# The opening of a decoder layer: one weight write earlier, GpSimd in program order, and the feed-forward buffers placed elsewhere

## The chip, the cores and the metric

The kernel runs on one core of a Trainium2 chip. The metric is the device time of one execution in microseconds, and a kernel's time is the median of its runs. TensorE (PE) multiplies matrices, VectorE (DVE), ScalarE (ACT) and GpSimd (POOL) work elementwise, and SyncE (SP) issues the transfers.

## The reference, cut to what matters

The input `x` has four time steps of 2048 items with 512 features, and there is a context of 77 rows for each of the four steps. Everything is in fp32. Three residual branches follow one another, each on a layer norm of x:

```python
def reference(x, ctx, ...):
    x = x + recurrence(layernorm(x), ...)      # 4 steps; z = V (A z + Vinv_dt u_t), per block of 64; 2 Re z
    x = x + cross_attention(layernorm(x), ctx, Wq, Wk, Wv, Wo)   # 16 heads of 32, 77 keys, softmax
    x = x + ffn(layernorm(x), ...)
    return x

def ffn(x, W_exp, b_exp, up_weights, up_bias, down_weights, W_con, b_con, down_bias):
    h = x @ W_exp + b_exp                      # 512 -> 2048
    h = butterfly(h, up_weights, 2048)         # 11 stages of 2x2 mixes
    h = gelu(h + up_bias)                      # exact
    h = butterfly(h, down_weights, 2048)
    return h @ W_con + b_con + down_bias       # 2048 -> 512
```

No weight meets a data-dependent value before the products, so the kernel composes each butterfly with its dense matrix once, and the recurrence of four steps becomes four fixed 64x64 taps.

## The kernel before, in words

**The rounds.** The 2048 items are worked in 16 groups of 128, each with its four time steps: 512 rows. `front(u)` makes the two norms, the recurrence and the attention of group u; `feed_forward(u)` makes its feed-forward part. After an opening, round u runs `feed_forward(u)`, and its `step()` calls draw pieces of `front(u+1)` in between, so that TensorE always has products of the one while the elementwise engines work on the other. The big products go by a seven-product scheme for 2x2 blocks: each matrix is kept as seven combinations of its quarters. There are seven for the query weights (`wq`, written to DRAM as `wq7`, and loaded again in every later round), seven for the output weights (`wo`, kept in SBUF), seven for each of eight column pieces p of the first feed-forward matrix (`up7[p]`), and seven arrays `dn7` for the second.

**The opening.** It prepares the operands and runs `front(0)`, and it is written as three generators that `run(...)` advances by hand in a fixed order:

- `_recurrence_taps` (L111 to L134) makes the taps `gt`: each step multiplies into a PSUM bank `ps_g` (then VectorE copies it out, L117), and into `ps_rr` and `ps_ri`, from which VectorE makes the next power. `_keys_values` (L140 to L160) loads the context `ct` and the weights `wk` and `wv`, multiplies the keys `ps_k` (L148; VectorE places them into `kbd`, L152) and the values `ps_v`.
- `_prepare` ("prep") composes the butterflies with the dense matrices. It regroups factors through DRAM (`hp_dn`, L218), multiplies diagonal pieces (L248 on VectorE), makes `wup`, the composed first matrix, and from its quarters the operands `up7[p]`: three of them are quarters as they are and are written straight from `wup` (L331, 24 DMA issues), four are sums made by two GpSimd and two VectorE operations for each p (L335 to L338) in a slot of the buffer `wo` (three slots, p % 3) and written from there (L339, eight DMA issues). Then the second matrix is composed into the same `wup` (L346, 16 groups of matmuls, each evicted by ScalarE or VectorE), transposed or multiplied on in the pairs L356 and L365, and its sums (L377 on VectorE and others) are written to `dn7`.
- `front(0)` ("first"): the norm (bn_stats; L469 on VectorE makes rows `xp`, L480 on TensorE transposes them into `ps_t`), the recurrence (L510), the second norm (L442 makes `xn`, L451 transposes), the query product (L495, whose partial sums VectorE adds in L532), the scores (L553), their softmax (L557, L558 on VectorE, L559 exp on ScalarE, L561 the sum, L563 the scaling on GpSimd), the transposes of the probabilities (L575 into `ps_pt`; the copies to SBUF, `pt`, by ScalarE in L578 and by VectorE in L580), the products with the values (L585) and with the output weights (L495 again, into `ps_w`), and the norm for the feed-forward.

**Buffers that are shared.** In SBUF `pt` has one buffer, and the query weights `wq` lie in the same one: it is free for the probabilities only when `wq` has been written out to `wq7` (L812) and the copy has landed. `wk` shares a buffer with `bd` of prep. The coefficients' pools (`prep`: `wup`, `wdn` and others) are released at the end of the opening, and the pools of the feed-forward (`ffn`, and `wts` with three buffers for weights in flight) are allocated after that. PSUM has eight banks named by tags; a new tile of a tag waits until the previous user of that bank has been read. `ps_g`, `ps_rr` and `ps_ri` all use tag f, as do the transposes and scores; prep uses a, b and c.

**What sets the order.** In the opening TensorE and SP run in program order (`tc.manual_schedule(engines={E.PE, E.SP})`); on the other engines, and on all of them in the rounds, a scheduler orders the instructions by when it thinks their inputs are ready. An engine works strictly through its queue: an instruction that waits stops what stands behind it. DMAs are issued from SP's queue, and take eight semaphores in turn, so each waits also for the one eight before it.

**Around the end of the opening.** The first weights `w_up` of the feed-forward are loaded at L663 and first used at L654. The operands of the right side, `tb` among them, are made by `combine` (L624, L625). The biases `ybias` are loaded and added on GpSimd (L830). In round 0 the first transposes L480 of `front(1)` come ahead of the first L654 in TensorE's queue.

Of the kernel before, what the change touches and what calls it, by code (L numbers as in the profile page):

```python
# [11 lines left out]
F32 = mybir.dt.float32  # L12
# [5 lines left out]
P = 128  # L18
# [49 lines left out]
def _recurrence_taps(nc, pool, psum, ssm_vec, ssm_vt, ssm_vinv, gt):  # L68
# [41 lines left out]
    for j in range(T):  # L110
        ps = psum.tile([P, 512], F32, tag="f", name="ps_g")  # L111
# [24 lines left out]
def _keys_values(nc, psum, ctx_t, wk_t, wv_t, kbd, vsb, room):  # L136
# [4 lines left out]
    nc.sync.dma_start(out=wk, in_=wk_t.rearrange("(c p) e -> p c e", p=P))  # L141
# [80 lines left out]
def _prepare(nc, keep, pool, room, late, banks, dram, ident, wexp_t, up_low, up_high, up_bias, dn_low, dn_high, wcon,  # L222
# [105 lines left out]
    for p in range(NB // 2):  # L328
        a11, a12, a21, a22 = quarters(p)
        for i, a in enumerate((a11, a12, a22)):  # L330
            nc.sync.dma_start(out=up7[p][:, i], in_=a)  # L331
    for p in range(NB // 2):
        a11, a12, a21, a22 = quarters(p)
        s = spare[:, p % 3 * 1024 : p % 3 * 1024 + 1024].rearrange("p (i k q) -> p i k q", i=4, k=k)
        nc.gpsimd.tensor_tensor(s[:, 0], a21, a22, ALU.add)  # L335
        nc.gpsimd.tensor_tensor(s[:, 2], a11, a21, ALU.subtract)
        nc.vector.tensor_tensor(s[:, 1], s[:, 0], a11, ALU.subtract)
        nc.vector.tensor_tensor(s[:, 3], a12, s[:, 1], ALU.subtract)  # L338
        nc.sync.dma_start(out=up7[p][:, 3:7], in_=s)  # L339
        yield  # L340
# [45 lines left out]
def kernel(ctx: ExitStack, tc: tile.TileContext, x, ctx_t, ssm_vec, ssm_vt, ssm_vinv, wq_t, wk_t, wv_t,  # L386
# [243 lines left out]
    def feed_forward(u, xt, rhs, other):  # L630
# [30 lines left out]
        def up_head(p):  # L661
            w = wts.tile([P, 7, 2, P], F32, tag="w", name="w_up")
# [12 lines left out]
        def up_mid(p):  # L675
            w, a, b, c, p1, u2 = live[p]
            up(p, 2, a, False)
            a11, a12, a21, a22, s1 = (ffn.tile([P, 2, P], F32, tag=g, bufs=h, name=g)
# [22 lines left out]
        for p in range(h):  # L701
            up_head(p)
            if p:
                up_tail(p - 1)
            up_mid(p)
# [10 lines left out]
        def down(i, ps, first):  # L716
            w = wts.tile([P, h, D // 2], F32, tag="w", name="w_dn")
# [15 lines left out]
        u2 = ffn.tile([P, 2, D // 2], F32, tag="u2d", bufs=1, name="u2d")  # L733
# [36 lines left out]
    with ExitStack() as stack, tc.manual_schedule(engines={E.PE, E.SP}):  # L770
# [37 lines left out]
        run(prep, first, prep, first, prep, first, prep)  # L808
        run(prep, prep, prep, prep)
        for _ in range(8):  # L810
            run(first, prep)
        nc.sync.dma_start(out=wq7, in_=wq)  # L812
        run(first, first, first)
        for n, _ in enumerate(prep):
            if n % 3 != 2 or n > 14:
                next(first, None)
# [14 lines left out]
    xlast = ctx.enter_context(tc.tile_pool(name="xlast", bufs=1))  # L831
    ffn = ctx.enter_context(tc.tile_pool(name="ffn", bufs=2))
    wts = ctx.enter_context(tc.tile_pool(name="wts", bufs=3))
# [75 lines left out]
```

## Time and profile before

| what | value |
|---|---|
| median of 3 runs | 2664.22 us (2663.57 to 2664.92) |
| profiled execution: its own time / its span | 2664.52 us / 2662.7 us |
| mean granted TensorE clock | 0.987 |
| busy: PE, DVE, ACT, POOL | 2570.4, 1453.5, 810.1, 949.7 us |
| moved by DMA | 333.60 MB |
| opening, to the first feed-forward matmul | 0 to 253.14 us |
| round 0, and each later round | 152.8 us, 150.5 us |

The profile shows one execution. Its span goes from the first instruction to the last, and the execution's own time is 1.8 us longer. The granted clock is the share of full speed at which TensorE was run: where it is 0.5, a matmul takes twice as long. In the views, "a <- b" behind a line says what an engine waited for and which instruction released it. "PEld" is the loading of weights into TensorE, which overlaps its multiplying.

### The profile page before, as it was taken

Reading aid. Unit: us, or ns where it says so; the run is one execution under the profiler, and the core shown is the slowest. Engines: PE = TensorE matmul, PEld = TensorE weight load, DVE = VectorE, ACT = ScalarE, POOL = GpSimd, SP = SyncE. Lnnn points to the kernel's source line nnn. Section 1 sums busy time; section 2 is a strip of 40 time slices with the busy share of each in tenths; the row PEclk is TensorE's granted clock in tenths of the full one; section 3 lists DMA queues with packets and bytes.
Section 4 is the critical chain, followed back from the end, with each engine's and each line's share of the span. In section 5 each row is a group of like instructions: output and inputs, shape, how many; then the busy total and the mean of one; then the engine's idle time right before and its main releaser. Section 6 shows DMA issues by size and latency. Waiting matters only on the chain.

```text
span 2662.7 us, 37427 instructions
## 1 busy us (share of the span) xinstructions
PE 2570.4 (97%) x14536; PEld 2183.1 (82%) x14536; DVE 1453.5 (55%) x3355; ACT 810.1 (30%) x1470; POOL 949.7 (36%) x1025
## 2 busy tenths in 40 slices
PE   7866999999999999999999999999999999999999
PEld 4755888888888888888888888888888888888888
DVE  6656554556455456546555555645555564554541
ACT  1422413324141332414133241413234141423420
POOL 4332251523434152333415243341524234252523
PEclk9987999999999999999999999999999999999999
DMA  5525324242332424233342424333242423323233
GB/s 175 170 99 188 132 86 148 96 167 96 122 131 102 148 81 171 94 130 120 105 145 98 154 94 156 109 105 131 97 164 85 165 99 114 136 98 136 96 130 139
DMA packets 94866, 333.60 MB, mean 125 GB/s; under 512 B 15585, under 2 KB 48481, under 8 KB 77537
## 3 DMA queue, kind: packets, MB, share of 16 engines
q1 hardware_dynamic: 94690, 331.21, 35.7%
q8 instruction: 116, 1.90, 0.3%
q14 instruction: 60, 0.49, 0.1%
HBM read 297.61 MB, written 33.57 MB: 124 GB/s over the span
## 4 chain that ended last, share of the span: by engine, by line
PE 83%; DVE 6%; ACT 4%; issue 1%; DMA 0%; POOL 0%; SPq 0%; ACTq 0%; DVEq 0%; POOLq 0%
PE ps_a L721 13%; PE ps_b L654 10%; PE ps_b L721 8%; PE ps_w L495 7%; PE ps_a L654 7%; PE ps_c L654 7%; PE ps_q L495 7%; PE ps_c L721 6%; PE ps_sc L553 5%; PE ps_pt L575 4%; PE ps_s L510 3%; PE ps_o L585 2%; PE ps_t L451 2%; ACT L559 1%; DVE st L416 1%
## 5 line engine op out<-in xcount | busy, mean ns | idle before, releaser
L654 PE MATMUL ps_b<-tb,w_up 128*128 128x256 f32 x1536 | 396.8, 379 | 0.0
L721 PE MATMUL ps_a<-w_dn,a 128*128 128x256 f32 x1536 | 373.0, 380 | 0.0
L697 POOL TENSOR_TENSOR s<-a,a 128x256 f32<-128x256 f32 x128 | 93.0, 727 | 676.4 <-ACT a L659 454.0
L654 PEld LDWEIGHTS ps_b<-tb,w_up 128*128 128x128 f32 x1536 | 287.4, 190 | 39.3
L659 ACT ACTIVATE a<-a,hbias 128x256 f32<-128x256 f32 x384 | 193.6, 508 | 409.3 <-DVE a L692 279.4
L721 PEld LDWEIGHTS ps_a<-w_dn,a 128*128 128x128 f32 x1536 | 282.4, 190 | 41.6 <-issue 3.0
L654 PE MATMUL ps_a<-xnt,w_up 128*128 128x256 f32 x1024 | 263.6, 380 | 0.0
L721 PE MATMUL ps_c<-w_dn,s 128*128 128x256 f32 x1024 | 248.6, 379 | 0.0
L563 POOL TENSOR_TENSOR pr<-pr,sm 128x1232 f32<-128x1232 f32 x64 | 144.0, 2250 | 263.0 <-DVE sm L562 259.0
L452 ACT COPY xnt<-ps_t 128x512 f32<-128x512 f32 x128 | 73.6, 587 | 522.7 <-PE ps_t L451 522.7
L654 PEld LDWEIGHTS ps_a<-xnt,w_up 128*128 128x128 f32 x1024 | 191.7, 191 | 25.7
L721 PEld LDWEIGHTS ps_c<-w_dn,s 128*128 128x128 f32 x1024 | 188.7, 190 | 27.8
L603 DVE TENSOR_TENSOR xt<-ps_w,xt 128x512 f32<-128x512 f32 x96 | 66.1, 689 | 214.5 <-PE ps_w L495 147.9
L709 POOL TENSOR_TENSOR xt<-xt,ybias 128x256 f32<-128x256 f32 x128 | 99.3, 810 | 223.0 <-DVE xn L442 222.9
L553 PE MATMUL ps_sc<-kbd,qt 128*128 128x308 f32 x512 | 172.6, 434 | 5.1 <-DVE pr L558 4.8
L575 PE MATMUL ps_pt<-ident,pr 128*77 128x128 f32 x1024 | 145.7, 278 | 29.0 <-ACT pt L578 17.8
L575 PEld LDWEIGHTS ps_pt<-ident,pr 128*77 128x77 f32 x1024 | 118.9, 149 | 61.7 <-ACT pt L578 26.4
L495 PE MATMUL ps_q<-xnt,wq 128*128 128x256 f32 x640 | 151.1, 379 | 0.5 <-issue 0.5
L559 ACT ACTIVATE pr<-pr 128x308 f32<-128x308 f32 x256 | 111.2, 457 | 131.5 <-DVE pr L558 131.0
L495 PEld LDWEIGHTS ps_q<-xnt,wq 128*128 128x128 f32 x640 | 121.4, 190 | 17.3 <-issue 0.8
L654 PE MATMUL ps_c<-xnt,w_up 128*128 128x256 f32 x512 | 131.5, 379 | 0.0
L654 PE MATMUL ps_c<-tb,w_up 128*128 128x256 f32 x512 | 131.5, 379 | 0.0
(199 smaller groups left out, 4513.0 us busy)
## 6 DMA issues: line engine op xcount, KB each, us to landing
w_up<-up SPq DMA_DIRECT2D x128, 896.0 KB, 4.6
w_dn<-dn SPq DMA_DIRECT2D x112, 1024.0 KB, 4.8
wq<-wq SPq DMA_DIRECT2D x16, 1792.0 KB, 8.7
xt<-in_x SPq DMA_DIRECT2D x16, 1024.0 KB, 5.2
out<-xt SPq DMA_DIRECT2D x64, 256.0 KB, 4.3
wdn<-in_wexp_t SPq DMA_DIRECT2D x4, 1024.0 KB, 10.4
wdn<-in_wcon SPq DMA_DIRECT2D x4, 1024.0 KB, 4.9
up<-wo SPq DMA_DIRECT2D x8, 512.0 KB, 2.7
```

Of the source, the lines that this page charges most:

```text
L452: nc.scalar.copy(xnt[:, :, t, :], ps)
L495: nc.tensor.matmul(tiles[key][:, r, :], lhsT=lhs(i, r, k), rhs=rhs(i, r, k), start=key == i and r == 0 and k == 0, stop=k == 1, skip_group ...
L510: nc.tensor.matmul(ps[:, 2 * i : T, f * NS : (f + 1) * NS], lhsT=xpt[:, i, c * (P // NS) + f, :], rhs=gt[:, 0 : T - 2 * i, :], start=i == ...
L553: nc.tensor.matmul(ps[:, 0 : 4 * NK], lhsT=qt[:, g, t, :], rhs=kbd[:, t, g, :], start=True, stop=True)
L559: nc.scalar.activation(pg, pg, AF.Exp, scale=1.0 / math.sqrt(DH))
L563: nc.gpsimd.tensor_tensor(pr, pr, sm.unsqueeze(2).to_broadcast([P, NH, NK]), ALU.mult)
L575: nc.tensor.transpose(pt_ps[0:NK, j, :], pr[:, 4 * g + j, :], ident)
L654: nc.tensor.matmul(ps, lhsT=w[:, c, :], rhs=rhs[i - 1][:, c], start=first and c == 0, stop=c == 1, skip_group_check=True)
L659: nc.scalar.activation(out, x, AF.Gelu, bias=hbias[:, b : b + 1])
L697: nc.gpsimd.tensor_tensor(s1, a21, a22, ALU.add)
L709: nc.gpsimd.tensor_tensor(r, r, ybias[:, d], ALU.add)
L721: nc.tensor.matmul(ps[:, t, :], lhsT=act[p][lhs[i]][:, t, :], rhs=w[:, p, :], start=first and p == 0 and t == 0, stop=p == h - 1, skip_gro ...
```

## The change

It has six parts, all about the opening and the first round:

1. `ps_g` moves from PSUM tag f to tag c, and `wk` is loaded in two halves of its columns.
2. Of the three quarters that go straight from `wup` to `up7`, only the first is written ahead of the sums; the other two (16 DMA issues) are written behind the last L339.
3. `wq7` is written right behind prep's first part, ahead of prep's loads of `wcon`, where it stood behind all the writes to `up7`.
4. GpSimd too runs in program order in the opening, and TensorE does in the first four pieces of round 0's feed-forward.
5. The hand-written turns of prep and first change: prep goes first in eight steps, one more step of prep comes early, and the steps of first behind that (second norm among them) are spread differently.
6. The feed-forward's operands `a11` to `s1` and `u2d`, and the weights' three buffers, are allocated in pools of their own: the operands at SBUF bytes 147136 to 190143 of a partition, two weight buffers at 190144 and 198336, `tb` and the rest at 206528, and the third weight buffer at 220864. Before, `ffn` came first and then one pool of three weight buffers.

The diff (some lines of unchanged context are left out):

```diff
@@ -1,5 +1,5 @@
 import math
-from contextlib import ExitStack
+from contextlib import ExitStack, nullcontext
 
 import numpy as np
 
@@ -108,7 +108,7 @@
     nc.vector.tensor_scalar(pz, pz, dt, None, ALU.mult)
     nc.gpsimd.memset(gt, 0.0)
     for j in range(T):
-        ps = psum.tile([P, 512], F32, tag="f", name="ps_g")
+        ps = psum.tile([P, 512], F32, tag="c", name="ps_g")
         nc.tensor.matmul(ps[:, 0:NS], lhsT=pz[:, 0, :], rhs=vt[:, 0, :], start=True, stop=False)
         nc.tensor.matmul(ps[:, 0:NS], lhsT=pz[:, 1, :], rhs=vt[:, 2, :], start=False, stop=True)
         for h in range(2):
@@ -138,7 +138,9 @@
 
     ct, wk, wv = room
     nc.sync.dma_start(out=ct, in_=ctx_t.rearrange("(c p) k -> p c k", p=P))
-    nc.sync.dma_start(out=wk, in_=wk_t.rearrange("(c p) e -> p c e", p=P))
+    for i in range(2):
+        q = slice(i * (D // 2), (i + 1) * (D // 2))
+        nc.sync.dma_start(out=wk[:, :, q], in_=wk_t.rearrange("(c p) e -> p c e", p=P)[:, :, q])
     yield
     nc.sync.dma_start(out=wv, in_=wv_t.rearrange("(c p) e -> p c e", p=P))
     yield
@@ -326,9 +328,7 @@
         return a11, a12, wup[:, 0:k, q], wup[:, k:NC, q]
 
     for p in range(NB // 2):
-        a11, a12, a21, a22 = quarters(p)
-        for i, a in enumerate((a11, a12, a22)):
-            nc.sync.dma_start(out=up7[p][:, i], in_=a)
+        nc.sync.dma_start(out=up7[p][:, 0], in_=quarters(p)[0])
     for p in range(NB // 2):
         a11, a12, a21, a22 = quarters(p)
         s = spare[:, p % 3 * 1024 : p % 3 * 1024 + 1024].rearrange("p (i k q) -> p i k q", i=4, k=k)
@@ -337,6 +337,10 @@
         nc.vector.tensor_tensor(s[:, 1], s[:, 0], a11, ALU.subtract)
         nc.vector.tensor_tensor(s[:, 3], a12, s[:, 1], ALU.subtract)
         nc.sync.dma_start(out=up7[p][:, 3:7], in_=s)
+        if p == NB // 2 - 1:
+            for n in range(NB // 2):
+                for i in (1, 2):
+                    nc.sync.dma_start(out=up7[n][:, i], in_=quarters(n)[2 * i - 1])
         yield
     nc.sync.dma_start(out=brow[1, :].rearrange("(p m) -> p m", m=NB), in_=b2)
     for c in range(NC):
@@ -659,7 +663,7 @@
             nc.scalar.activation(out, x, AF.Gelu, bias=hbias[:, b : b + 1])
 
         def up_head(p):
-            w = wts.tile([P, 7, 2, P], F32, tag="w", name="w_up")
+            w = weights([P, 7, 2, P], "w_up")
             nc.sync.dma_start(out=w, in_=up7[p])
             a, b, c = (bank(g).rearrange("p (x t q) -> p x t q", x=2, q=P)[:, 0] for g in "abc")
             live[p] = (w, a, b, c)
@@ -675,7 +679,7 @@
         def up_mid(p):
             w, a, b, c, p1, u2 = live[p]
             up(p, 2, a, False)
-            a11, a12, a21, a22, s1 = (ffn.tile([P, 2, P], F32, tag=g, bufs=h, name=g)
+            a11, a12, a21, a22, s1 = (acts.tile([P, 2, P], F32, tag=g, name=g)
                                       for g in ("a11", "a12", "a21", "a22", "s1"))
             gelu(a11, a, p)
             up(p, 7, b, False)
@@ -699,10 +703,11 @@
             del live[p]
 
         for p in range(h):
-            up_head(p)
-            if p:
-                up_tail(p - 1)
-            up_mid(p)
+            with tc.manual_schedule(engines={mybir.EngineType.PE}) if u == 0 and p < 4 else nullcontext():
+                up_head(p)
+                if p:
+                    up_tail(p - 1)
+                up_mid(p)
             if p == 1 and u + 2 < NU:
                 xts[u + 2] = load_x(u + 2)
             r, d = xt[:, p // 2, p % 2 * (D // 2) : (p % 2 + 1) * (D // 2)], slice(p % 2 * (D // 2), (p % 2 + 1) * (D // 2))
@@ -714,7 +719,7 @@
         r11, r12, r21, r22 = (xt[:, t : t + 2, d : d + D // 2] for t in (0, 2) for d in (0, D // 2))
 
         def down(i, ps, first):
-            w = wts.tile([P, h, D // 2], F32, tag="w", name="w_dn")
+            w = weights([P, h, D // 2], "w_dn")
             nc.sync.dma_start(out=w, in_=dn7[i - 1])
             for p in range(h):
                 for t in range(2):
@@ -730,7 +735,7 @@
         for p in range(h):
             nc.gpsimd.tensor_tensor(act[p][4], act[p][4], act[p][0], ALU.subtract)
         down(1, a, True)
-        u2 = ffn.tile([P, 2, D // 2], F32, tag="u2d", bufs=1, name="u2d")
+        u2 = acts.tile([P, 2, D // 2], F32, tag="u2d", bufs=1, name="u2d")
         nc.scalar.copy(u2, a)
         down(6, b, True)
         nc.vector.tensor_tensor(u2, b, u2, ALU.add)
@@ -767,7 +772,7 @@
     xts = {}
     ready = []
     E = mybir.EngineType
-    with ExitStack() as stack, tc.manual_schedule(engines={E.PE, E.SP}):
+    with ExitStack() as stack, tc.manual_schedule(engines={E.PE, E.SP, E.Pool}):
         pool = stack.enter_context(tc.tile_pool(name="prep", bufs=1))
         wup = pool.tile([P, NC, HID], F32, name="wup")
         wdn = pool.tile([P, NB, D], F32, name="wdn")
@@ -806,13 +811,13 @@
         nc.gpsimd.tensor_tensor(wq[:, 2], wq[:, 1], wq[:, 5], ALU.subtract)
         run(prep, prep, first, prep, first, prep, first)
         run(prep, first, prep, first, prep, first, prep)
+        nc.sync.dma_start(out=wq7, in_=wq)
         run(prep, prep, prep, prep)
         for _ in range(8):
-            run(first, prep)
-        nc.sync.dma_start(out=wq7, in_=wq)
-        run(first, first, first)
+            run(prep, first)
+        run(first, first)
         for n, _ in enumerate(prep):
-            if n % 3 != 2 or n > 14:
+            if n not in (3, 6, 9, 12, 23, 24, 25, 26):
                 next(first, None)
             if n == 3:
                 quarter_loads(wo, wo_t, (0, 1, 2, 6))
@@ -829,8 +834,16 @@
         nc.sync.dma_start(out=db, in_=down_bias.partition_broadcast(P))
         nc.gpsimd.tensor_tensor(ybias, ybias, db, ALU.add)
     xlast = ctx.enter_context(tc.tile_pool(name="xlast", bufs=1))
+    acts = ctx.enter_context(tc.tile_pool(name="acts", bufs=NB // 2))
+    wts = [ctx.enter_context(tc.tile_pool(name=f"wts{i}", bufs=1)) for i in range(2)]
     ffn = ctx.enter_context(tc.tile_pool(name="ffn", bufs=2))
-    wts = ctx.enter_context(tc.tile_pool(name="wts", bufs=3))
+    wts.append(ctx.enter_context(tc.tile_pool(name="wts2", bufs=1)))
+    loaded = [0]
+
+    def weights(shape, name):
+        loaded[0] += 1
+        return wts[loaded[0] % 3 - 2].tile(shape, F32, tag="w", name=name)
+
     combine(ready[0][2], ready)
     for u in range(NU):
         other = front(u + 1, xts.pop(u + 1), ready) if u + 1 < NU else iter(())
```

## The prediction

> **What bounds the kernel now.** I read the page's busy row first: TensorE is busy for 97% of the span, so nothing in the sixteen rounds is worth much unless it shortens TensorE's own work. The slices say where the other 3% lie: the first four of forty are below 9 and the clock dips there.
>
> ```profile
> PE 2570.4 (97%) x14536; PEld 2183.1 (82%) x14536; DVE 1453.5 (55%) x3355; ACT 810.1 (30%) x1470; POOL 949.7 (36%) x1025
> ...
> PE   7866999999999999999999999999999999999999
> ...
> PEclk9987999999999999999999999999999999999999
> ```
>
> Then busy time by stretch (span; PE, PEld, DVE, ACT, POOL busy; granted clock; DMA share; GB/s): the opening up to the first feed-forward matmul at 253.14, cut into five stages, and the first two rounds.
>
> ```profile
> 0.00:58.00 58.00, 42.47 (x146) 24.28 (x147) 33.16 (x119) 5.75 (x10) 28.94 (x82) 0.91 0.60 201
> 58.00:107.00 49.00, 47.80 (x416) 45.89 (x415) 27.30 (x64) 25.76 (x38) 12.35 (x10) 1.00 0.35 114
> 107.00:154.00 47.00, 21.05 (x82) 14.45 (x81) 29.65 (x60) 6.13 (x11) 16.22 (x17) 0.73 0.72 241
> 154.00:208.00 54.00, 48.89 (x409) 40.60 (x409) 30.79 (x49) 17.38 (x33) 18.81 (x13) 0.98 0.10 36
> 208.00:253.10 45.10, 24.76 (x100) 16.16 (x99) 33.15 (x77) 11.77 (x21) 13.61 (x13) 0.71 0.73 228
> ...
> 253.00:405.80 152.80, 151.47 (x848) 129.31 (x848) 83.41 (x193) 46.39 (x85) 56.39 (x59) 0.99 0.32 112
> 405.80:556.30 150.50, 149.17 (x850) 127.44 (x849) 85.55 (x198) 48.40 (x88) 55.53 (x57) 1.00 0.35 122
> ```
>
> A round has 1.3 us without TensorE; the stages 0 to 58, 107 to 154 and 208 to 253 have 15.5, 26.0 and 20.3. What can be won lies in those 62 us. TensorE's waits of the first 400 us name it, and the timeline shows the largest:
>
> ```profile
> PE ps_pt L575 <- ACT pt L578: 17.8, 3, 16.3
> PE ps_t L480 <- DVE xp L469: 13.6, 4, 7.7
> PE ps_k L148 <- DMA wk<-in_wk_t: 10.0, 1, 10.0
> PE ps_t L451 <- DVE xn L442: 7.7, 2, 6.7
> PE ps_ri L124 <- DVE gt L117: 5.2, 3, 2.3
> ...
> 122.17 21.45 SPq L339 DMA_DIRECT2D up<-wo  x8
> ...
> 143.66 0.44 SPq L812 DMA_DIRECT2D wq<-wq  x1
> ...
> 151.44 0.69 DVE L580 COPY pt<-ps_pt 77x512 f32<-77x512 f32 x1 [8.21 <-DMA wq<-wq]
> ...
> 152.12 1.99 PE L575 MATMUL ps_pt<-ident,pr 128*77 128x128 f32 x8 [16.30 <-ACT pt L578]
> ...
> 242.56 0.80 SPq L663 DMA_DIRECT2D w_up<-up  x2
> ...
> 253.14 1.76 PE L654 MATMUL ps_a<-xnt,w_up 128*128 128x256 f32 x4
> ```
>
> The transposed probabilities (pt) take the buffer of the query weights (wq). Their copy waits until wq has been written out; that write stands on the SP queue behind 24 issues of L331 and 8 of L339, is issued at 143.66 and lands 7.7 us later. Below, lines and times are those of before.
>
> **The change, part by part.** One caution on all: where stages follow one another, a shift won in one is carried on only while TensorE, and not a transfer, is what the next waits for.
>
> *Taps' banks and halves of wk (0 to 58).* With the power sums ps_g in tag c, ps_ri no longer takes the bank that L117 must empty: the three waits of 5.2 us go. The first eight ps_k passes need one half of wk. The context landed at 6.9 (2.62 + 4.3), all of wk at 9.9; I put the half at 8.4. SP has one issue of 0.5 us more, and everything behind lands later by that (wv 18.0, used 34.3; x 21.4, used 25.1: covered). VectorE's new order puts four bn_stats (0.65 each) behind the key copies instead of beside matmuls. Walk: ps_k 8.4 to 15.6, three products unhindered to 18.0, ps_k to 20.3, second tap 21.2 to 23.1 (L131 stands behind one key copy), ps_k to 25.4, or 27.2 at half clock, third tap to 29.6, ps_v 3.4 to 33.0, fourth tap at 35 (behind the bn_stats), ps_v 7.1, so the transposes L480 start near 42 instead of 48.02. Bounds 0 and -7; I take -5.5. From 58 to 107 TensorE is busy 98% in an unchanged order, so it is carried on.
>
> *wq written early, and the pieces of the first feed-forward matrix (107 to 154).* The write moves on SP to a place behind the regrouped factors (L218, 87.76) and ahead of the four wcon loads (first at 93.03). wq is final when L806 ends (44.2), so SP doesn't wait. Its 7.7 us fall where DMA is at 0.55; wcon may land 3 us later, but is first read past 130. L331 shrinks from 24 issues to 8 ahead of the L339 writes; the other 16 (0.63 us each) come behind them.
>
> With the wq wait gone, what is late next is VectorE with GpSimd, now in program order. Walk, without the shift of the first part: VectorE's 16 diagonals L248 (0.29 us, 0.40 beside GpSimd) all stand ahead of the query addition L532, which ends at 114.5 instead of 111.5; TensorE's seventh query product waits 3.8 instead of 0.93 us, loses its clock, and the last L532 ends near 125 instead of 120.2. In the scores VectorE alternates L557/L558 (0.48) with the pieces L337/L338 (0.41 alone, 0.93 beside GpSimd). A piece needs its slot of three back: L338, SP, landing (2.7, at most 4.5). Pieces 3 to 6 come at about 1.5 us of GpSimd apart, their slots free in time. L561 of the first probabilities starts near 134 (124.9 before), L563 ends near 137 and the last pair L335/L336 1.5 later; VectorE's last L337 frees the last score bank for the transposes and lets ScalarE's first eviction of L346 go, behind which the last exp waits. So L585 starts near 143 instead of 154.04: -11. TensorE comes out of the thin stretch about 3 us closer to its half clock than before, which costs 1. Take -10. From below: each of five pieces waiting for a 4.5 us landing, 1.8 over the median, and dearer pieces give back 6: -4. From above: no lost clock and pieces always at 0.41: -14.
>
> Covered: the 16 late writes are issued until 150 and landed by 153; the first eviction that overwrites what they read is the ninth group of L346, near 163 (174 before, less 11). The wo loads behind them land by 157 and are combined by 162; ps_w needs them at 176.
>
> *One L346 group earlier* fills waiting time: -0.4.
>
> *The norm's transposes later (208 to 238).* L451 stood among the L356/L365 pairs and held them up for 6.7 us until VectorE had the statistics. Moved behind, the pairs run on at 1.29 us each, and VectorE becomes the bound: from 207.75 to L377's end at 237.54 it idled 3.9 us, its work is the same. -3.9, between -1 (its evictions wait for TensorE) and -4.5.
>
> *Operands and first weights elsewhere in SBUF.* In the built program's lists of waits, the first w_up load and the first tb still name the last dn7 writes, as before, though the addresses no longer meet: the release of the coefficients' pool is one event for all. Cost and gain 0; were the wait gone, 242.56 would be 240.8, so at most -1.8.
>
> *First transposes of round 1 behind the first feed-forward matmul.* Before, L480 waited for VectorE, which waited for the biases (L830), and L654 stood behind it at 253.14, though the weights had landed 6.8 us after 242.56. Now it starts at 249.4: -3.7. It must be paid back: 16 transposes (0.11 each) and two L510 (0.18) move into round 0, which TensorE fills: +2.1.
>
> *Clock at the start of round 0.* The trace: full clock came at 254.65, after a window filled with L480 and two L510 and little else; so L654 lost 0.75. The Trainium skill, "TensorE: Matmul & The Clock Gate", section "Part 4: PE-mode transpose", says that transposes do not count as busy for the gate. By that rule L480 had warmed nothing, and moving it costs no clock: +0. The trace speaks against it (mean clock 0.56 from 252 to 255), and measurement decides: with nothing ahead of L654 the clock stays at half for the rest of one window and a full next one. That page's section "Part 1: The HAM clock gate" gives windows of about 3.4 us; 4.2 us passed here from 151.5 to full clock, 6.0 from 221.4. Estimate 5 us at half speed, 2.5 lost: +1.7.
>
> Sum: -5.5 - 10 - 0.4 - 3.9 - 3.7 + 2.1 + 1.7 = -19.7. From the profiled execution's 2664.5 (span 2662.7 and 1.8 around it) this makes 2644.8; its time is 0.3 above the median of the runs, 2664.22. I say 2645.
>
> **The rivals.**
>
> *VectorE takes the wait over.* Its queue now holds diagonals, pieces and scores in one order. If pieces run at 0.93 and the slots wait, 107 to 154 brings 4 instead of 10; if bn_stats hold the fourth tap, the first part brings 2; the tail brings 2: -2 - 4 - 0.4 - 2 - 3.7 + 3.8 = -8.3, 2656. For it: VectorE and GpSimd already alternate at 129 to 143. Against: even so no wait of 16 us is in reach. Chance 0.15.
>
> *It does what its title says.* The weights load ahead of the release, or taps and pieces run free: the upper bounds, to -28, 2637. Against: the wait lists. Chance 0.08.
>
> *Nothing measurable*, given back in round 0: program order for TensorE while p < 4 makes each wait for VectorE stop TensorE, and that round had only 1.4 us of them. To lose 15 us it must stall at most of its 16 steps. Chance 0.04.
>
> *Slower: the new places cost every round.* tb, a11 to s1 and the weight ring have other addresses in all 16 rounds, and the ring is three pools of one buffer. If a load had to wait longer or an access ran slower there, each round would grow. To come out slower by 0.2% it takes 25 us over 16 rounds, 1.6 us on 150.5; at 2 us the time is 2677. Against: the waits of w_up and w_dn name the same transfers and matmuls, the order from the middle of round 0 is unchanged, and no row shows a duration that goes with an address. Chance 0.05.
>
> The main case has 0.68. A measurement can tell 0.2% (5.3 us) from no change. Faster: 0.68 + 0.15 + 0.08 = 0.91; same 0.04; slower 0.05. The range 2637 to 2656 reaches to the first two rivals.
>
> **What would show it.** Right: no wait of ps_ri for gt; L480 near 42; the wq write near 83, no wait of pt for it; L585 of the first probabilities near 137 (143 less 5.5); L654 near 230; round 0 some 4 us longer, the others at 150.5. Wrong: L585 later than 145; TensorE waits for L532 or L558 that together pass 12 us; L654 later than 238; rounds 1 to 15 other than 150.5.

## The result

The changed kernel takes 2640.69 us (median of 4 runs, 2638.80 to 2643.37), the kernel before 2664.57 (4 runs). The ratio is 0.9912, 95% interval 0.9895 to 0.9929: 23.9 us less, where 19.7 less was forecast (2645, range 2637 to 2656). The profiled execution took 2640.16 us with a span of 2638.4. From here on, lines of the changed kernel are its own: up to 5 more than before.

The page of the changed kernel, first the busy row, then TensorE and its granted clock in 40 slices:

```profile
PE 2566.2 (97%) x14536; PEld 2182.0 (83%) x14536; DVE 1449.0 (55%) x3355; ACT 809.9 (31%) x1470; POOL 950.1 (36%) x1025
...
PE   7887999999999999999999999999999999999999
...
PEclk9898999999999999999999999999999999999999
```

TensorE does the same 14536 matmuls; its busy time fell by 4 us, while its mean granted clock rose from 0.987 to 0.993. The rest of the gain is idle time. The same stages as in the prediction, cut where the same work begins (span; PE, PEld, DVE, ACT, POOL busy; clock; DMA share; GB/s):

```profile
0.00:52.10 52.10, 38.21 (x146) 23.09 (x147) 33.41 (x119) 5.96 (x10) 29.80 (x82) 0.97 0.68 223
52.10:101.10 49.00, 47.81 (x417) 45.90 (x415) 27.28 (x64) 25.75 (x38) 10.39 (x7) 1.00 0.44 151
101.10:136.20 35.10, 24.26 (x91) 17.23 (x90) 27.73 (x60) 7.12 (x13) 15.23 (x18) 0.81 0.51 182
136.20:189.80 53.60, 48.38 (x406) 40.15 (x407) 31.91 (x53) 16.67 (x31) 21.06 (x14) 1.00 0.33 101
189.80:224.50 34.70, 17.70 (x76) 10.28 (x74) 26.70 (x69) 9.08 (x16) 8.92 (x6) 0.84 0.73 231
224.50:381.50 157.00, 155.65 (x864) 132.68 (x865) 86.81 (x199) 48.37 (x88) 61.25 (x66) 0.98 0.34 121
381.50:532.00 150.50, 149.17 (x850) 127.45 (x849) 85.53 (x198) 48.40 (x88) 55.54 (x57) 1.00 0.34 121
```

The three thin stages lost 5.9, 11.9 and 10.4 us. Round 0 took 4.2 more, and a later round takes 150.5 as before. TensorE's waits of the first 400 us:

```profile
PE ps_a L658 <- DMA w_up<-up: 12.0, 1, 12.0
PE ps_k L150 <- DMA wk<-in_wk_t: 9.1, 1, 9.1
PE ps_sc L557 <- DVE pr L562: 5.7, 7, 1.0
PE ps_t L455 <- DVE xn L446: 5.4, 2, 4.5
PE ps_q L499 <- DVE qt L536: 5.1, 1, 5.1
PE ps_t L484 <- DVE xp L473: 2.9, 2, 2.0
PE ps_pt L579 <- ACT pt L582: 1.5, 2, 0.7
```

The wait of the probabilities for `wq` (16.3 us) and those of `ps_ri` (5.2) are gone. A new one heads the list: the first feed-forward product waits 12.0 us for its weights. The timeline shows both ends:

```profile
83.08 0.43 SPq L814 DMA_DIRECT2D wq<-wq  x1
...
219.45 0.80 SPq L667 DMA_DIRECT2D w_up<-up  x2
...
224.55 2.04 PE L658 MATMUL ps_a<-xnt,w_up 128*128 128x256 f32 x4 [11.97 <-DMA w_up<-up]
226.39 1.91 PE L658 MATMUL ps_b<-tb,w_up 128*128 128x256 f32 x4
228.10 1.91 PE L658 MATMUL ps_c<-tb,w_up 128*128 128x256 f32 x4
229.80 1.44 PE L658 MATMUL ps_a<-xnt,w_up 128*128 128x256 f32 x4
231.08 1.03 PE L658 MATMUL ps_b<-tb,w_up 128*128 128x256 f32 x4
```

Read the starts: groups of four begin 1.7 us apart until 229.80, and 0.86 apart from 231.94 on. The clock is at half from 217.0 to 230.6, as a window out of that stretch shows (clock in the last column but two):

```profile
218.00:230.60 12.60, 6.05 (x14) 4.88 (x15) 4.40 (x5) 1.66 (x2) 9.89 (x11) 0.50 0.93 349
```

Of the 12.0 us, 6.9 pass before SP issues the load (TensorE's last matmul before it ends at 212.6), and 5.1 from there to the first product.

### The profile page after: what moved, and what is told of

The parts are those of the page before. It is cut to its first block, busy times and chain, and to the rows that moved or that the text cites. A ratio compares the mean times of both kernels' runs of the same rounds, so it can differ in the third digit from the quotient of the medians.

```text
span 2638.4 us, 37437 instructions
## 1 busy us (share of the span) xinstructions
PE 2566.2 (97%) x14536; PEld 2182.0 (83%) x14536; DVE 1449.0 (55%) x3355; ACT 809.9 (31%) x1470; POOL 950.1 (36%) x1025
## 4 chain that ended last, share of the span: by engine, by line
PE 83%; DVE 6%; ACT 5%; issue 1%; DMA 0%; ACTq 0%; DVEq 0%; SPq 0%
PE ps_a L726 13%; PE ps_b L658 10%; PE ps_b L726 8%; PE ps_w L499 7%; PE ps_a L658 7%; PE ps_c L658 7%; PE ps_q L499 7%; PE ps_c L726 6%; PE ps_sc L557 5%; PE ps_pt L579 4%; PE ps_s L514 3%; PE ps_o L589 2%; PE ps_t L455 2%; ACT L563 1%; ACT L663 1%; DVE st L420 1%
## 5 line engine op out<-in xcount | busy, mean ns | idle before, releaser
L658 PE MATMUL ps_b<-tb,w_up 128*128 128x256 f32 x1536 | 397.7, 380 | 0.0
L658 PEld LDWEIGHTS ps_b<-tb,w_up 128*128 128x128 f32 x1536 | 287.7, 190 | 39.4
L658 PE MATMUL ps_a<-xnt,w_up 128*128 128x256 f32 x1024 | 264.2, 381 | 12.0 <-DMA w_up<-up 12.0
L658 PEld LDWEIGHTS ps_a<-xnt,w_up 128*128 128x128 f32 x1024 | 192.0, 191 | 37.9 <-issue 12.2
L563 ACT ACTIVATE pr<-pr 128x308 f32<-128x308 f32 x256 | 111.1, 457 | 136.2 <-DVE pr L562 135.7
L672 ACT COPY p<-ps_a 128x256 f32<-128x256 f32 x128 | 47.7, 373 | 277.7 <-PE ps_a L658 277.7
L658 PE MATMUL ps_c<-tb,w_up 128*128 128x256 f32 x512 | 132.5, 381 | 0.0
```

Source lines behind the costliest of these rows:

```text
L563: nc.scalar.activation(pg, pg, AF.Exp, scale=1.0 / math.sqrt(DH))
L658: nc.tensor.matmul(ps, lhsT=w[:, c, :], rhs=rhs[i - 1][:, c], start=first and c == 0, stop=c == 1, skip_group_check=True)
```

## The experiments

Each kernel in this table is one part of the change away from one of the two; the last one adds two edits of its own. The table holds, from each profile, when TensorE begins a stage (us from the span's start; "products" is the first product with the values, L585 before), and what lies between the first feed-forward matmul and the end of the span; the last column is the median of the runs. Differences in the text are taken before rounding.

| kernel | query | scores | products | ps_w | first feed-forward | from there to the end | median |
|---|---|---|---|---|---|---|---|
| before | 85.8 | 119.3 | 154.0 | 187.7 | 253.1 | 2409.6 | 2664.2 |
| changed | 79.8 | 119.2 | 136.2 | 169.3 | 224.6 | 2413.8 | 2640.7 |
| before + wq early | 83.9 | 117.5 | 136.5 | 173.9 | 238.4 | 2409.6 | 2650.7 |
| before + taps | 82.1 | 115.7 | 150.4 | 185.4 | 249.5 | 2409.6 | 2660.8 |
| changed, wq late | 82.7 | 121.8 | 155.6 | 191.4 | 247.5 | 2413.8 | 2660.9 |
| changed, no taps | 85.4 | 125.1 | 141.9 | 174.9 | 232.8 | 2413.1 | 2647.6 |
| changed, old pools | 77.9 | 117.2 | 134.4 | 167.5 | 224.8 | 2412.7 | 2639.8 |
| changed, GpSimd's order free | 80.8 | 118.1 | 136.1 | 169.1 | 225.5 | 2412.7 | 2639.9 |
| changed, TensorE's order free | 78.1 | 117.2 | 134.5 | 167.6 | 228.2 | 2408.7 | 2639.9 |
| changed, first ahead of prep | 78.8 | 117.3 | 137.3 | 170.3 | 227.0 | 2413.6 | 2644.3 |
| changed, weights really early | 78.4 | 117.7 | 134.9 | 167.9 | 211.1 | 2417.5 | 2630.1 |

The query column differs by up to 5 us among kernels whose code is the same up to there. The reason is shown below under the taps, and stages are therefore compared by differences within a row.

**The write of wq, alone.** To the kernel before:

```diff
         run(prep, first, prep, first, prep, first, prep)
+        nc.sync.dma_start(out=wq7, in_=wq)
         run(prep, prep, prep, prep)
         for _ in range(8):
             run(first, prep)
-        nc.sync.dma_start(out=wq7, in_=wq)
```

> The kernel before with one edit: the write of wq to wq7 stands behind prep's first part, as in the changed kernel. Theory (this write carries half of the gain): the 16.3 us wait of the probabilities' transposes for wq goes; next late is VectorE with its pieces of the first matrix, which here still stand behind 24 plain writes. First product with the values near 140 instead of 154.0, carried to the end: -10 to -14, 2651 to 2655. Rival (VectorE takes the wait over at once, since L580 is queued behind the last piece at 143): -8 or less, 2656 or more.

Measured: 2650.71 us, ratio 0.9951 (0.9938 to 0.9965), 13.5 less. Its waits of TensorE between 130 and 260 us name no wait for `wq`, and the rest is unchanged:

```profile
PE ps_t L480 <- DVE xp L469: 13.6, 4, 7.6
...
PE ps_pt L575 <- DVE pr L558: 4.3, 1, 4.3
...
PE ps_pt L575 <- ACT pt L578: 1.5, 2, 0.7
```

From the query product to `ps_w` it needs 90.0 us, the kernel before 102.0 and the changed one 89.4. So the moved write alone carries 12.0 of this stage's 12.6 us. The products begin earlier here than in the changed kernel, counted from the query product (52.6 against 56.4 us), yet `ps_w` does not gain by it. From the first product to `ps_w` TensorE has the same 304 matmuls in all kernels of the table (a view counts one or two more at its edges), but needs 37.4 us here and 33.1 in the changed kernel. The clock makes the difference; two views of this kernel, then one of the changed one:

```profile
136.48:146.90 10.42, 9.37 (x54) 6.97 (x55) 7.36 (x12) 1.45 (x4) 3.52 (x3) 0.50 0.68 235
146.90:173.87 26.97, 23.05 (x252) 20.19 (x251) 16.64 (x28) 9.95 (x19) 11.36 (x8) 1.00 0.01 3
...
136.20:169.26 33.06, 27.98 (x305) 24.05 (x305) 20.36 (x38) 10.80 (x21) 13.67 (x9) 1.00 0.33 95
```

In the first 10.4 us TensorE is busy for 9.4 at half clock; at full clock that work would take 4.7 less (an estimate by halving), and 4.3 is the difference. So the changed kernel, whose scores come 5.8 us later behind the query product, gets most of that back here, by a warmer clock.

**The write of wq, undone in the changed kernel.** It stands behind the eight joint turns:

```diff
-        nc.sync.dma_start(out=wq7, in_=wq)
         run(prep, prep, prep, prep)
         for _ in range(8):
             run(prep, first)
+        nc.sync.dma_start(out=wq7, in_=wq)
```

> The changed kernel with one part undone: wq is written behind prep's and first's eight joint turns, so behind all writes of the first matrix. Theory: the write is issued near 143 and lands near 151.5, so the first product with the values starts near 152 instead of 136.2; everything behind it follows TensorE and VectorE, so +14 to +16: 2655 to 2657. Rival (pieces and VectorE bound this stage, not wq): within 3 us of the changed kernel, 2641 to 2644.

Measured: 2660.85 us, 20.2 more than the changed kernel, and above the range. The wait is back, 16.6 us long (16.3 in the kernel before):

```profile
PE ps_pt L579 <- ACT pt L582: 18.1, 3, 16.6
```

From the query product to the first product with the values it takes 72.9 us instead of 56.4: 16.6 more, where the theory had 14 to 16 for everything. The excess lies at the clock: from the first product with the values to `ps_w` it takes 35.8 us instead of 33.1, since here the first 5.7 us run at half.

```profile
155.61:161.30 5.69, 5.69 (x45) 4.27 (x44) 1.86 (x3) 0.58 (x1) 0.00 (x0) 0.50 0.00 0
```

Its query product also began 2.8 us later than in the changed kernel's profile, by the variation of the first 60 us (this profile's own time, 2663.16 us, is the longest of its twelve runs); the rival is out by far.

**The taps' banks and the halves of wk, alone and undone.** Alone, in the kernel before:

```diff
-        ps = psum.tile([P, 512], F32, tag="f", name="ps_g")
+        ps = psum.tile([P, 512], F32, tag="c", name="ps_g")
...
-    nc.sync.dma_start(out=wk, in_=wk_t.rearrange("(c p) e -> p c e", p=P))
+    for i in range(2):
+        q = slice(i * (D // 2), (i + 1) * (D // 2))
+        nc.sync.dma_start(out=wk[:, :, q], in_=wk_t.rearrange("(c p) e -> p c e", p=P)[:, :, q])
```

> The kernel before with one edit: ps_g in tag c and wk loaded in two halves. Theory: the first transposes of the norm start near 38 to 42 instead of 48.0, prep's pieces and with them all writes on SP come some 6 us earlier, and the gain is carried to the end: -5 to -6.5, 2658 to 2659.5. Rival (given back in the scores, as the changed kernel's first score at 119.2 against 119.3 suggests): 0 to -1, 2663.5 to 2664.5.

The same edit the other way round, in the changed kernel:

> The changed kernel with one part undone: ps_g in tag f and wk in one load, as before. Theory (the 5.2 us of waits come back and every later stage follows): the query product starts near 84 to 86 instead of 78 to 83, +3.3 (what this part alone brought) to +6: 2644 to 2646.7. Rival (the later stage is bound by VectorE from its own start, and swallows it): within 1 us of the changed kernel, 2640 to 2642.

Measured: alone 2660.83 us, ratio 0.9987 (0.9981 to 0.9994), 3.3 less; undone 2647.64, 6.9 more than the changed kernel. Carried to the end in both, so the rivals fall; the two sizes lie on either side of the ranges. The reason for the first is in the windows of the kernel with the taps alone:

```profile
46.00:49.00 3.00, 1.80 (x7) 1.64 (x8) 1.05 (x1) 0.59 (x1) 0.91 (x1) 0.50 0.00 0
49.00:52.00 3.00, 3.00 (x12) 2.63 (x11) 0.69 (x1) 0.00 (x0) 0.00 (x0) 0.50 0.00 0
```

and of the changed kernel with the weights really early, whose instructions have the changed kernel's order up to there:

```profile
46.00:49.00 3.00, 3.00 (x20) 2.80 (x21) 0.69 (x1) 0.59 (x1) 2.24 (x2) 1.00 0.00 0
```

The norm's first transposes come 10 us earlier (37.5 and 37.8 instead of 48.0), and then TensorE waits for VectorE's next rows, at the longest 1.3 to 3.8 us. How much of the gain the clock takes back differs from profile to profile. Eleven profiles hold this edit, with the same order of instructions on TensorE up to the query product. Five have no half-clock window in the first 60 us and reach the query product at 77.9 to 79.1 us (longest wait 1.3 to 1.9 us); four have one and reach it at 79.7 to 80.8 (2.0 to 2.8 us); two have two windows and reach it at 82.1 and 82.7. The kernel with the taps alone is one of these two, so its 3.6 us at the query product are what is left of more. Its 21 runs fall into four from 2656.7 to 2658.5 and seventeen from 2659.8 to 2662.3; the mean granted clock is 0.989 or 0.990 in the four and 0.988 or 0.989 in the seventeen. That fits fewer such windows in the four, but only one of the runs, out of the seventeen, has a profile.

Undone, the query product comes 5.6 us later. A further 2.6 us come between `ps_w` and the first feed-forward product, 1.7 of them because the first weights were 6.6 us on their way instead of 5.0; why a load takes longer in one profile than in another stays open.

**The places in SBUF.** The changed kernel with the two pools of before; no instruction changes its place in any queue:

```diff
-    acts = ctx.enter_context(tc.tile_pool(name="acts", bufs=NB // 2))
-    wts = [ctx.enter_context(tc.tile_pool(name=f"wts{i}", bufs=1)) for i in range(2)]
     ffn = ctx.enter_context(tc.tile_pool(name="ffn", bufs=2))
-    wts.append(ctx.enter_context(tc.tile_pool(name="wts2", bufs=1)))
+    wts = ctx.enter_context(tc.tile_pool(name="wts", bufs=3))
```

> The changed kernel with one part undone: operands and weights are allocated in the two pools of the kernel before; the order of instructions on every engine is that of the changed kernel. Theory: the first weights wait for the same release in both, so nothing changes: within 1.5 us of the changed kernel's 2640.7. Rival (the new places do something): the first weights arrive later, +1.8 or more, 2642.5 or more; or, if the new places cost in every round, 2639 or less.

Measured: 2639.82 us, 0.9 below the changed kernel and inside its runs' spread. The new places bring nothing and cost nothing that these runs can tell. The first weights were 7.0 us on their way in this profile and 5.0 in the changed kernel's, which looks like the rival; but with the new places and the same order on SP they took 6.4 and 6.7 in the two kernels below that have useless work on TensorE.

**GpSimd's order.** The changed kernel with `manual_schedule(engines={E.PE, E.SP})`:

> The changed kernel with one part undone: GpSimd's order in the opening is the scheduler's; of the other engines only eight softmax instructions of VectorE stand elsewhere. Theory (the fixed order carries nothing by itself, wq's early write does): within 2 us of the changed kernel, 2639 to 2643. Rival (it is what keeps the sums of the first matrix from waiting): first product with the values at 140 or later instead of 136.2, +4 or more, 2645.

Measured: 2639.86 us, 0.8 below. The last VectorE piece L338 starts at 127.7 instead of 133.3, and the first product with the values at 136.1 instead of 136.2: the order carries nothing, though the title of the change names it.

**TensorE's order in round 0.** The changed kernel without `manual_schedule` for p < 4:

> The changed kernel with one part undone: TensorE's order in round 0 is the scheduler's, so the four transposes of round 1 (L484) and two L514 stand ahead of the first L658 again. Theory of the prediction (an earlier first product, paid back by moved transposes and a colder clock): first L658 near 230 instead of 224.6, what follows it shorter by some 4.2 us, together 0 to +2: 2640 to 2643. Rival (program order there is a gain of its own, as the wait for VectorE is off the path): +4 or more, 2645.

Measured: 2639.90 us, 0.8 below. The timeline has the transposes in front again:

```profile
222.19 1.09 PE L484 MATMUL ps_t<-ident,xp 128*128 128x128 f32 x4 [7.09 <-DVE xp L473]
...
227.34 1.06 PE L514 MATMUL ps_s<-gt,xpt 128*128 128x256 f32 x2
228.20 1.15 PE L658 MATMUL ps_a<-xnt,w_up 128*128 128x256 f32 x4
229.18 1.03 PE L658 MATMUL ps_b<-tb,w_up 128*128 128x256 f32 x4
```

The first L658 comes 3.6 us later than in the changed kernel, and 5.1 are saved behind it: no clock is lost (groups 0.9 us apart at once) and the transposes are done. The edit is neutral, as the theory says.

**The flip of prep and first.** From the scores' column I suspected that the flip had given back the 5.9 us between query product and scores. The changed kernel with `run(first, prep)` in the eight turns:

> The changed kernel with one part undone: in the eight joint turns first goes ahead of prep again. On VectorE one query addition L536 then stands ahead of the last seven diagonals and none behind all sixteen; TensorE and SP keep their order. Theory (the flip is the step that gave back 5.9 us between the query product and the scores): first score near 113.5 instead of 119.2 where the opening runs alike, first product with the values near 131 to 133 instead of 136.2, -3 to -5: 2635.5 to 2637.5. Rival (the sums of the first matrix bound the stage, so an earlier score only waits longer for VectorE): within 1 us of the changed kernel.

Measured: 2644.26 us (2641.20 to 2647.76), 3.6 more. The theory falls, and the rival, within 1 us, is not met either. VectorE's timeline shows why the score did not come earlier:

```profile
107.34 0.94 DVE L337 TENSOR_TENSOR wo<-wo,wup 128x256 f32<-128x256 f32 x1 [1.85 <-POOL wo L335]
108.20 1.81 DVE L338 TENSOR_TENSOR wo<-wup,wo 128x256 f32<-128x256 f32 x2
...
110.28 0.68 DVE L536 TENSOR_TENSOR qt<-ps_q,qt 128x512 f32<-128x512 f32 x1
```

The query addition L536 no longer stands behind all sixteen diagonals, but behind pieces that wait for GpSimd: one wait has taken the other's place, and the scores begin 38.5 us behind the query product instead of 39.4. The first product with the values follows them 20.0 us later instead of 17.0, so the old order costs 2.1 us up to there. With wq early in the kernel before the scores begin 33.6 us behind the query product. GpSimd's free order brings it to 37.4 in its profile, with one half-clock window ahead of the scores instead of two; which edit the rest belongs to was not tried.

**The weights really ahead.** The built program's waits said that the first weights wait for the release of the coefficients' pool. Here `up7[0]` and `up7[1]` go into a buffer that is free before, and the small coefficients lie in a pool of their own:

```diff
             if n == 18:
                 xts[1] = load_x(1)
+                head = work.tile([P, 2, 7, 2, P], F32, tag="pt", bufs=1, name="w_head")
+                for i in range(2):
+                    nc.sync.dma_start(out=head[:, i], in_=up7[i])
...
-            w = weights([P, 7, 2, P], "w_up")
-            nc.sync.dma_start(out=w, in_=up7[p])
+            if u == 0 and p < 2:
+                w = head[:, p]
+            else:
+                w = weights([P, 7, 2, P], "w_up")
+                nc.sync.dma_start(out=w, in_=up7[p])
...
+        small_pool = stack.enter_context(tc.tile_pool(name="prep2", bufs=1))
-        prep = _prepare(nc, tc.keep_in_program_order, pool, rooms, ...)
+        prep = _prepare(nc, tc.keep_in_program_order, small_pool, rooms, ...)
```

> The changed kernel with the first weights really loaded ahead: up7[0] and up7[1] go into the buffer of the probabilities (free after the last L584) at the 19th turn, and the coefficients lie in two pools, so that the operands tb and p1 wait for the low coefficients only and no longer for the last writes of dn7. Theory (the 12.0 us wait of the first L658 is the release, not the bandwidth): first L658 at 213, then a stop for tb until 216.5, pieces run on; -5 to -9: 2632 to 2636. Rival (the gelu's outputs a11 still lie over wup and wait for the last write's landing near 219, so TensorE stops at its second piece): -2 to -4, 2637 to 2639.

Measured: 2630.11 us, ratio to before 0.9870 (0.9855 to 0.9885): 10.6 below the changed kernel, a little beyond the theory's range, and the fastest of all kernels here. Its timeline:

```profile
211.10 1.89 PE L658 MATMUL ps_a<-xnt,w_head 128*128 128x256 f32 x8
214.75 1.63 DVE L630 TENSOR_TENSOR tb<-xnt,tb 128x512 f32<-128x512 f32 x1
...
216.48 2.05 PE L658 MATMUL ps_b<-tb,w_head 128*128 128x256 f32 x4 [3.49 <-issue]
218.32 1.91 PE L658 MATMUL ps_c<-tb,w_head 128*128 128x256 f32 x4
```

The first product starts at 211.1 and stops until 216.48, as expected: the profile names no releaser, but VectorE's last write to `tb` ends 0.1 us before. It does not stop for the gelu's outputs. Of the 12.0 us wait, the 6.9 before the issue went by until the last sum was made (2.6) and the pool was released behind its writes (4.3); the 5.1 on the way are gone too, since this load, issued at 171.2 and landed at 182.1, is ahead of its use by 29 us. How much the weights' buffer and the second pool bring each was not tried. Four L658 are still 1.7 us apart up to 221.73: the clock is at half for the second stretch.

**The clock at the first L658.** The changed kernel with useless work in TensorE's queue where it waits 12.0 us, first transposes, then plain products:

```diff
         for _ in first:
             pass
+        fill = psum.tile([P, 512], F32, tag="f", name="ps_fill")
+        for _ in range(88):
+            nc.tensor.transpose(fill[:, 0:P], ident, ident)    # or: nc.tensor.matmul(fill[:, 0:P], lhsT=ident, rhs=ident, ...)
```

> The changed kernel with 88 transposes of the identity into a PSUM bank that nobody reads, in TensorE's queue between the last transposes of the norm and the first L658, where it waits 12.0 us for the weights. They need 9.5 us at full clock (0.108 each, from L484) and 14 if the clock falls on the way. Theory (transposes keep the clock, as in the kernel before, where they were nearly all that ran ahead of the full clock): first L658 still near 224.5, four of its matmuls at once 0.87 us apart instead of 1.71, -2 to -3: 2637.5 to 2639. Rival ([...]transposes do not count as busy): clock at half from about 218, the transposes end near 225 to 227, L658 at half clock for 6 us again: 0 to +3, 2641 to 2644.

> As the kernel with 88 transposes, with 88 plain products of the identity with itself in their place, of the same shape. Both theories expect the full clock at the first L658 and -2 to -3: 2637.5 to 2639. If this one gains nothing either, the 3.1 us that the first sixteen L658 lose are not the clock's (a rival: their weights are still landing).

Measured: 2640.70 us with transposes, 2644.98 with products. Neither gives the 2 to 3 us, but the timelines settle the question of the clock. With transposes, two views (timeline; then windows with the clock in the last column but two):

```profile
213.14 9.77 PE L834 MATMUL ps_fill<-ident 128*128 128x128 f32 x88
226.76 1.12 PE L658 MATMUL ps_a<-xnt,w_up 128*128 128x256 f32 x4 [3.85 <-DMA w_up<-up]
227.70 1.89 PE L658 MATMUL ps_b<-tb,w_up 128*128 128x256 f32 x4
```

```profile
218.00:221.00 3.00, 3.00 (x29) 3.00 (x28) 0.51 (x1) 0.00 (x0) 0.51 (x1) 1.00 0.86 248
221.00:224.00 3.00, 1.91 (x18) 1.67 (x16) 1.83 (x2) 0.00 (x0) 2.37 (x2) 1.00 0.93 314
224.00:227.00 3.00, 0.24 (x1) 0.27 (x2) 1.53 (x2) 0.00 (x0) 2.92 (x5) 1.00 0.97 371
```

All 88 transposes ran 0.11 us apart, and the clock stayed at full until 227.7, where the changed kernel has it at half from 217.0. The fill ended at 222.9, 3.85 us ahead of the weights; that gap cost one window (at half from 227.7 to 231.1, groups of L658 1.7 us apart from 227.70 to 231.09). From the first L658 to the end it takes 2412.5 us instead of 2413.8; that the median is no better is the weights' way again, 6.4 us here instead of 5.0. With products:

```profile
212.76 19.82 PE L834 MATMUL ps_fill<-ident 128*128 128x128 f32 x176
232.42 1.03 PE L658 MATMUL ps_a<-xnt,w_up 128*128 128x256 f32 x4
```

A plain fp32 product is two matmul records of 0.113 us, a transpose is one: the fill ran 19.8 us and held L658 up. But the groups are 0.86 us apart from the first, and from the first L658 to the end it takes 2410.8 us instead of 2413.8. So the 3.1 us that the first sixteen L658 lose are the clock's. These products by themselves leave the rival cause, weights that still land, since they start some 6 us after the landing; the transposes put it out: there L658 starts 0.1 us after its weights land, its first group runs at full pace (0.94 us to the next), and the pace halves and doubles where the clock does.

**Both gaps filled.** The kernel with the weights early, with 40 and 36 such products in its two last gaps:

> The kernel with the first weights loaded ahead and the coefficients in two pools, and plain products of the identity in its two last idle stretches: 40 ahead of the first L455 (4.5 us idle) and 36 between the first two groups of L658 (3.5 us idle). Theory (both stretches cost a window at half clock, 3.4 us of records behind the first and 6.8 behind the second): -3 to -4.5 against 2630.1, 2625.5 to 2627. Rival (VectorE bounds the stretch behind the first gap, and products that outlast a gap are paid in full): -1 to +1, 2629 to 2631.

Measured: 2638.30 us, 8.2 more than without the fill, outside both ranges. The size was wrong by that factor of two:

```profile
200.51 9.09 PE L831 MATMUL ps_fill<-ident 128*128 128x128 f32 x80
...
215.07 8.20 PE L679 MATMUL ps_fill<-ident 128*128 128x128 f32 x72
```

Gaps of 4.5 and 3.5 us were filled with 9.1 and 8.2. The fill did keep the clock: the half-clock windows at 205 to 209 and 215 to 222 are gone, and the next comes at 229.6. What a fill of the right size would give was not tried.

## Why the prediction was right, point by point

- **Taps.** Forecast -5.5; the query product came 5.9 us earlier in the profile, and the part is worth 3.3 us alone and 6.9 in company. The gain is carried on, as the walk assumed. The first L480 at 37.8 was outside the bound that was given (-7 from 48.0); the excess went back into TensorE's wait for VectorE (2.9 us) and into the clock, and the walk had not followed the stage beyond its first transposes. That the term nevertheless came near is in part luck: the same code reaches the query product at 77.9 to 82.7, by the number of half-clock windows.
- **The wq write.** Forecast -10 for its stage, with a cost of 1 us for a colder clock in it. Measured -11.9 from query product to first product with the values (68.3 to 56.4 us), and no clock was lost behind it (1.00 from 136 to 190). The walk's points held: the last query addition ended at 120.1 (walked: 125 less the first part's 5.5), the first product with the values came at 136.2 (137.5). TensorE's wait for L536 was 5.1 us, walked at 3.8, and the clock was at half from 107.7 to 114.6. The edit alone gives 13.5 us of run time, and undone it costs 20.2: it is the largest part. GpSimd's order adds nothing that these runs can tell. The flip, undone, costs 3.6 us. The split of L331 was not tried alone.
- **One L346 group earlier.** Forecast -0.4; it can't be told apart. From first product to `ps_w` 33.7 us became 33.1, but with the same 304 matmuls, and the kernel before runs the first 1.6 us of them at half clock. The `ps_w` stage, which has the group less, took 0.3 us more.
- **The norm's transposes later.** Forecast -3.9; from the end of the `ps_w` stage to the last sum L377 it took 29.5 us before and 25.4 after: -4.2. This part was not tried alone.
- **SBUF places.** Forecast 0; -0.9 when undone, inside the spread.
- **First L654 earlier, moved transposes, clock.** Forecast -3.7 + 2.1 + 1.7. Measured: last sum to first feed-forward matmul 15.6 to 9.4 us, so -6.2. The mis-sized term is the weights' way: they were issued 4.3 us behind the last sum instead of 5.0, and landed 5.0 us later instead of 6.8, figures that the prediction had taken over from before. The shorter landing was in part the luck of this profile: with the same order of issues on SP up to there it took 6.4, 6.7 and 7.0 us in three others. Round 0 grew by 4.2 instead of 3.8: 1.7 us for the four groups of transposes and 0.4 for two L514, which is the forecast 2.1, and 3.1 - 0.7 = 2.4 for the clock (sixteen L658 in 6.5 us instead of 3.5; before, the first four lost 0.7), together 0.3 more than was measured. The clock stayed at half for 6.1 us behind the first L658, where 5 were estimated. The rule of the Trainium skill that was weighed against this, "TensorE: Matmul & The Clock Gate", section "Part 4: PE-mode transpose", is contradicted here for fp32 transposes of 128x128: 88 of them alone held full clock for 9.8 us. By it the move would have cost no clock. Its windows of about 3.4 us (section "Part 1: The HAM clock gate") fit what was seen, a single gap of 3.85 us costing one window of 3.4.

The sum by the profile is -5.9 - 11.9 - 0.6 + 0.3 - 4.2 - 6.2 + 4.2 = -24.3, the amount by which the span is shorter; the +0.3 is the `ps_w` stage itself. The forecast was 4.6 us short, 2.5 of them in the weights' way and 1.9 in the wq stage. The rivals: VectorE does take over part of the wait (5.1 us for L536), but at a length that was nearly in the sum already; that the places in SBUF cost every round is excluded, since rounds take 150.5 us.

## What to carry to other kernels

In an order written by hand, look first for a transfer that something late waits for and that stands behind others it has nothing to do with: one moved line gave 13.5 of 23.9 us by itself. Where a stall is removed, follow the stage to its next wait and to the clock behind it, since a shift of ten microseconds at one instruction was worth six some instructions later and, run alone, three. And when a new wait heads the list, ask what releases it: the first weights could not be loaded before a pool of buffers was released, and loading them into a buffer that was free, with the coefficients in two pools, gave another 10.6 us.

## What the runs showed of the hardware that was not expected

- Fp32 transposes of 128x128 keep TensorE's clock up (1.00 through 9.8 us of nothing else; without them it fell to 0.50 some 4.4 us after the last matmul).
- A plain 128x128x128 fp32 product appears as two matmuls and takes 0.225 us, a transpose of the same tile as one and takes 0.111.
- The same code runs its first 60 us in times that differ by some 5 us (query product from 77.9 to 82.7 among the kernels that contain the taps' edit), with zero, one or two half-clock windows of 3.4 us, each costing about half its length. With changes of this size the stages of two profiles are compared by differences, and only medians of several runs tell kernels apart.
- The clock reaches further than the wait that cooled it. The same 304 matmuls from the first product with the values to `ps_w` take 33.1 us where the clock is full from their start, 33.7 to 35.8 with 1.6 to 5.7 us at half, and 37.4 with 10.4 us at half.
